# A planned kernel for four graph layers: a new VectorE-GpSimd lock and a new transfer queue in the planner, with new stage times

## The chip, the cores and the metric

The kernel runs on one NeuronCore of a Trainium2 chip. Its engines run side by side, each with its own queue of instructions served in order: TensorE (PE in the profile, its weight loads PEld), VectorE (DVE), ScalarE (ACT), GpSimd (POOL), and SyncE (SP), which here issues nearly all transfers. The metric is the device time of one execution in microseconds (us), as a median of runs. The kernel before took 2754.69 us (median of 3, from 2750.09 to 2756.34).

## The reference

There are 128 graphs of 128 nodes with 256 features (`x`, float32) and an integer adjacency matrix each (`adj`). Four layers follow, each inside `x = layernorm(x + layer(x, adj))`:

```
layer 0   e_k = leaky_relu((x * a_k) @ x.T), k = 0..3; alpha = softmax(e_k where adj == k+1, else -9e15); alpha @ x
layer 1   relu(x @ W_upd + mean over incoming edges of (x @ W_msg) + bias)
layer 2   three times: m = h @ weight[i]; agg = (adj != 0).T @ m; h = GRU(agg, h)
layer 3   Wh = x @ W; e = leaky_relu(f_i + f_j); softmax over edges; elu(alpha @ Wh)
```

The GRU's gates are `r = sigmoid(i_r + h_r)`, `z = sigmoid(i_z + h_z)`, `n = tanh(i_n + r * h_n)` and `h = (1 - z) * n + z * h`. All is float32.

## The kernel before

Graphs are taken in 32 groups of four, so that most tiles are 128 partitions by 512 columns. A group passes the stages `loading`, `layer0`, `layer1`, `step0`, `step1`, `step2` (the three GRU steps) and `layer3`. The gate products of the GRU use a seven-product scheme on two-by-two blocks (`gate`, line 753), the sums for it being made by `sums` (line 731): on GpSimd for the hidden state (`t_h`) and on VectorE for the aggregate (`t_m`). ScalarE and VectorE take the partial results out of PSUM (`q`, `t_r`, `t_i`, `t_z`). Transposes go mostly through VectorE's blockwise transpose into `z`, one transfer to DRAM (`turn`, line 487) and four transfers back (`back`, line 492): this is how `probT`, `x1T`, `hT`, `hn`, `rT` and `xc` come about. Layer norms use `statistics` (line 519): VectorE makes mean and variance, adds epsilon (`rstd`, four columns), GpSimd raises it to the power -0.5 (`rstd` again), and VectorE makes `shift`, also four columns. `normalise` then runs mostly on ScalarE.

No operation is issued as it is written. Every call is recorded as an `Op` (`Engine.__getattr__`, line 186) with its buffers, its dependences, a duration from a cost function for its engine (`pe_cost` to `sp_cost`, lines 244 to 280), and `lasts`, after which its result can be read. A planner, at the end of the function, then imitates the machine: it keeps a time at which each engine is free, asks `start_of` (line 1005) when each ready operation could start, takes the engine that can start first, and among its operations that could start by then issues the one with the earliest due time. All instructions of the main part are therefore issued from line 228, which is the line that the profile names for nearly everything.

The due times (`nominal`) come from `paced` (line 330): group g's stage lies at g times `PERIOD` plus a pair in `TIMES`, moved by a table `HEAD` for the first six groups and `TAIL` for the last six. A stage's due times are spread evenly over its operations. `EAGER` and `RUSH` move urgent operations ahead. Due times only rank operations: the planner never waits for one. About six groups are in flight at a time, since a group's stages reach from about 250 us before to 240 us after its own multiple of `PERIOD`.

Two rules of the planner stand at the centre of the change. The first is a lock between VectorE and GpSimd. An operation with `holds` set keeps the other engine's `holds` operations from starting until shortly before its end (`held`, lines 1008 and 1052). Before, VectorE's operations hold if neither output nor a wide input is in PSUM and they have two inputs of more than four columns, or are of the `FAST` forms (tensor_scalar and kin) with an output of more than four columns; `rstd`, `shift` and `ninv`, with four columns, do not. GpSimd's hold if they are a memset or have two inputs of more than four columns. The second is the landing of a transfer: a constant by tile from `LANDING` (2.4 us if not listed), plus `DMA_SLACK`, counted from its issue, whatever else is in the queue.

Of the kernel before, what the change touches and what calls it, by code (L numbers as in the profile page):

```python
# [18 lines left out]
def kernel(  # L19
# [54 lines left out]
    psum = ctx.enter_context(tc.tile_pool(name="psum", bufs=4, space=bass.MemoryType.PSUM))  # L74
# [68 lines left out]
    def m_of(view):  # L143

        m = 1
        for d in view.shape[1:]:
            m *= d
        return m
# [3 lines left out]

    class Op:
        def __init__(self, engine):
            self.engine, self.calls, self.took, self.lasts, self.dma = engine, [], 0.0, 0.0, False
            self.after, self.bufs, self.waiting = {}, [], 0
            self.ready, self.nominal, self.urgent = 0.0, 0.0, False
            self.holds = False
            self.rush = 0.0

    class Engine:
# [24 lines left out]
        def __getattr__(self, name):  # L186
            def call(*args, **kw):
                op = self.group or self.record()
                named = dict(kw)
                out = [named.pop("out")] if "out" in named else [args[0]]  # L190
                rest = args if "out" in kw else args[1:]
                if "accum_out" in named:
                    out.append(named.pop("accum_out"))
                out = [v for v in out if isinstance(v, View)]
                ins = [v for v in (*rest, *named.values()) if isinstance(v, View)]
                n = max([m_of(v) for v in out + ins])
                tensors = [v for v in ins if m_of(v) > 4]
                took, lasts = self.cost(name, n, out, ins, len(ins) - len(tensors), "accum_out" in kw)
                op.lasts = op.took + lasts
                op.took += took  # L200
                op.dma = name == "dma_start"
                if self is POOL:
                    op.holds = name == "memset" or len(tensors) > 1
                elif self is DVE and name not in ("transpose", "bn_stats"):
                    op.holds = not any(v.buf.pool is psum for v in out + tensors) and (
                        len(tensors) > 1 or (name in FAST and m_of(out[0]) > 4)
                    )
                for views, writes in ((ins, False), (out, True)):
                    for v in views:
                        whole = v.buf.pool is psum  # L210
                        for other, box, wrote in v.buf.accesses:
                            if other is not op and (writes or wrote) and (
                                whole or all(a < d and c < b for (a, b), (c, d) in zip(box, v.box))
                            ):
                                other.after[id(op)] = op
                for views, writes in ((ins, False), (out, True)):
                    for v in views:
                        v.buf.accesses.append((op, v.box, writes))
                        if v.buf not in op.bufs:
                            op.bufs.append(v.buf)  # L220
                            v.buf.left += 1
                op.calls.append((name, args, kw))

            return call
# [8 lines left out]


    FAST = ("tensor_scalar", "tensor_scalar_add", "tensor_scalar_mul")
    LANDING = {"e": 5.66, "adj_in": 4.0, "x_in": 3.85, "x1T": 3.53, "way_1": 3.2, "way_2": 3.0, "xc": 3.6, "way_f": 2.0}

    def tag_of(v):
        return v.buf.tag

    def in_psum(views):
        return any(v.buf.pool is psum for v in views)
# [16 lines left out]

    def act_cost(op, n, out, ins, pointers, sums):  # L260
        if op == "dma_start":
            return 0.6, 5.0
        lasts = 0.162 + n * 0.00083 + 0.1 * pointers
        return lasts - 0.104 + (0.12 if sums else 0.0), lasts + (0.11 if sums else 0.0)

# [11 lines left out]
        return (1.2, 1.2) if n <= 256 else (2.2, 2.2)  # L277

    def sp_cost(op, n, out, ins, pointers, sums):
        return 0.55, LANDING.get(tag_of(out[0]) if out else "out", 2.4)  # L280

    PE = Engine("PE", nc.tensor, pe_cost)
    DVE = Engine("DVE", nc.vector, dve_cost)
# [3 lines left out]
    engines = (PE, DVE, ACT, POOL, SP)  # L287


    PERIOD = 81.83483  # L290
    EAGER, RUSH = 5.2365, 0.7497
    HOP, PE_HOP, SLACK, DMA_SLACK = 0.0946, 0.0838, 0.2615, 1.3152
    STAGES = ("loading", "layer0", "layer1", "step0", "step1", "step2", "layer3")
    TIMES = {
        "loading": ((-253.2780, -231.9501), (-180.9657, -182.6682),),
        "layer0": ((-168.5025, -107.0697),),
        "layer1": ((-62.6359, -4.7662),),
        "step0": ((-4.4948, 10.3141), (7.8309, 27.7350), (15.3585, 41.6638),),
        "step1": ((53.6280, 63.7962), (55.4424, 67.5800), (69.3938, 96.3237),),
        "step2": ((107.5318, 125.3405), (123.0192, 128.3402), (118.3669, 151.8864),),  # L300
        "layer3": ((179.8537, 241.5793),),
    }
    HEAD = (
        (-47.114, 18.617, -36.138, -28.741, -1.314, -6.344, -10.582),
        (24.334, 50.812, 17.569, -15.154, 21.237, -1.480, -6.111),
        (8.991, 0.482, 19.681, -1.325, -6.604, -1.406, -2.988),
        (-25.999, 20.490, 6.185, 5.893, -23.153, 10.547, -15.132),
        (-68.952, -1.643, -3.814, -2.005, -11.556, 1.656, 4.907),
        (153.035, -10.082, -1.797, 2.074, -6.131, -2.621, -1.970),
    )  # L310
    TAIL = (
        (-25.939, 2.926, -0.338, -2.915, -0.707, 12.085, 19.318),
        (-15.615, 8.572, 14.121, 0.973, -4.836, -7.460, 3.775),
        (16.695, 22.604, 4.276, 8.937, -5.182, 2.007, 1.764),
        (-11.456, -21.112, 0.381, -6.411, -11.631, 3.563, -8.765),
        (-90.353, -2.307, -9.971, -4.006, 15.211, 6.428, 6.000),
        (82.599, 6.878, -1.456, 4.198, -5.620, 19.044, 23.289),
    )

    def spread(start, end, pe_only=False):  # L320
# [684 lines left out]
    def start_of(op):  # L1005

        at = op.ready
        if op.holds:
            at = max(at, (POOL if op.engine is DVE else DVE).held)
        for buf in op.bufs:  # L1010
            if buf.tile is None:
                slot = slot_at(buf)
                if slot is None:
                    return None
                at = max(at, slot + HOP)
                if buf.pool is psum:

                    for other, _, _ in buf.accesses:
                        for b in other.bufs:
                            if other is not op and b.tile is None and b is not buf and slot_at(b, True) is None:  # L1020
                                return None
        return at
# [5 lines left out]
    while left:  # L1028
        best = None
        for e in engines:  # L1030
            starts = [(start_of(op), op) for op in e.ready]
            starts = [(at, op) for at, op in starts if at is not None]
            if not starts:
                continue
            at = max(e.free, min(at for at, op in starts))
            if best is None or at < best[0]:
                op = min(
                    (op for t, op in starts if t <= at),
                    key=lambda op: op.nominal - (EAGER if op.urgent and e is not PE else 0.0) - op.rush * RUSH,
                )  # L1040
                best = (at, op)
        at, op = best
        e = op.engine
        for buf in op.bufs:
            if buf.tile is None:
                take_slot(buf)
        e.issue(op)
        e.ready.remove(op)
        e.free = at + op.took
        end = at + op.lasts + (DMA_SLACK if op.dma else 0.0)  # L1050
        if op.holds:
            e.held = at + op.lasts - 0.12
        for buf in op.bufs:
            buf.left -= 1
            buf.free_at = max(buf.free_at, end)
        for other in op.after.values():
            other.waiting -= 1
            to_pe = other.engine is PE
            if e is PE and to_pe:
                ready = e.free  # L1060
            elif e is other.engine and not op.dma:
                ready = end
            else:
                ready = end + (SLACK if not other.urgent else PE_HOP if to_pe else HOP)
            other.ready = max(other.ready, ready)
            if other.waiting == 0:
                other.engine.ready.append(other)
        left -= 1
# [28 lines left out]
```

## Time and profile before

| | |
|---|---|
| median of three runs | 2754.69 us (2750.09 to 2756.34) |
| profiled execution | 2750.87 us |
| its span, first to last instruction | 2749.0 us |
| mean granted TensorE clock | 0.994 |
| TensorE busy | 2678.5 us (97%), 14,332 matmul records |
| VectorE busy | 2183.6 us (79%) |
| ScalarE busy | 1807.6 us (66%) |
| GpSimd busy | 1570.5 us (57%) |
| transfers | 288.37 MB, queue q1 busy for 50.4% of 16 engines' span |

A float32 matmul is two records, a bfloat16 one is one. Matmuls are pipelined and their ends are modelled, so that TensorE's busy share is an upper figure. In groups such as `shift<-mv,rstd`, names are tiles without their numbers, left of the arrow what is written; after the count come busy time and mean duration, then the idle time of the engine before them. In the list of waits, the columns are total time, number and longest. A wait for several semaphores is put down to the last.

### The profile page before, as it was taken

The numbers are of one execution on the slowest core, as the hardware profiler recorded it, in microseconds if no ns is written. First come the engines' busy times: TensorE is split into PE (matmuls) and PEld (weight loads), VectorE is DVE, ScalarE is ACT, GpSimd is POOL, SyncE is SP. The second block draws the span as 40 slices with busy tenths as digits, with TensorE's granted clock in tenths as the row PEclk, the third lists the DMA queues.
The fourth block names the chain that finished last, engine by engine and source line by source line (L and its number), as shares of the span: only waits on it lengthen the run. The fifth ranks groups of instructions, "written<-read, shape, count | busy, mean of one in ns | idle before, by whom it ended". The sixth has DMA issues, their size and how long they took to land. (4 is left out here: it accounts for less than half of the span.)

```text
span 2749.0 us, 45121 instructions
## 1 busy us (share of the span) xinstructions
PE 2678.5 (97%) x14332; PEld 2232.4 (81%) x14332; DVE 2183.6 (79%) x5044; ACT 1807.6 (66%) x4336; POOL 1570.5 (57%) x1546
## 2 busy tenths in 40 slices
PE   8999999999999999999999999999999999999995
PEld 5788888888888888888888888888887888887784
DVE  5777878778788877788878788878778888778875
ACT  3556666666666666766666676666766666666665
POOL 4555656555656555666555657555566555566542
PEclk9999999999999999999999999999999999999997
DMA  5545555545545555555555545555545546354432
GB/s 114 112 88 108 104 102 116 110 98 105 110 105 116 109 108 101 110 112 116 115 109 104 110 106 119 117 106 110 103 105 112 113 96 132 79 105 89 99 71 51
DMA packets 1385661, 288.37 MB, mean 105 GB/s; under 512 B 1139408, under 2 KB 1385296, under 8 KB 1385424
## 3 DMA queue, kind: packets, MB, share of 16 engines
q1 hardware_dynamic: 1382976, 283.13, 50.4%
q10 hardware_dynamic: 2448, 2.36, 0.3%
q8 instruction: 115, 1.88, 0.3%
q14 instruction: 122, 1.00, 0.1%
HBM read 168.96 MB, written 116.38 MB: 104 GB/s over the span
## 5 line engine op out<-in xcount | busy, mean ns | idle before, releaser
L228 POOL TENSOR_TENSOR t_r<-t_r,t_i 128x512 f32<-128x512 f32 x186 | 244.4, 1324 | 280.8 <-ACT t_i L228 207.5
L228 PE MATMUL gate<-t_h,w_hhT 128*128 128x256 f32 x1152 | 348.1, 386 | 5.9 <-ACT t_z L228 3.8
L228 PE MATMUL gate<-t_h,w_sh 128*128 128x256 f32 x1152 | 342.0, 383 | 4.1 <-ACT q L228 1.7
L228 PE MATMUL gate<-t_m,w_sm 128*128 128x256 f32 x1152 | 341.5, 380 | 1.0 <-DVE t_m L228 0.5
L228 PE MATMUL gate<-agT,c_gi 128*128 128x256 f32 x1152 | 340.3, 380 | 1.6 <-ACT t_z L228 0.6
L228 PE MATMUL gate<-t_m,c_gi 128*128 128x256 f32 x1152 | 340.4, 379 | 0.0
L228 PE MATMUL gate<-hT,w_hhT 128*128 128x256 f32 x1152 | 331.1, 382 | 3.9 <-ACT t_z L228 2.0
L228 POOL TENSOR_TENSOR t_d<-hT,t_n 128x512 f32<-128x512 f32 x192 | 250.8, 1319 | 45.1 <-ACT t_n L228 44.5
L228 PEld LDWEIGHTS gate<-t_h,w_hhT 128*128 128x128 f32 x1152 | 207.8, 190 | 63.8 <-issue 19.8
L228 PEld LDWEIGHTS ps<-xs,xT 128*128 128x128 f32 x2048 | 248.0, 192 | 13.4 <-ACT xs L228 3.7
L228 PE MATMUL ps<-xs,xT 128*128 128x128 f32 x2048 | 251.4, 275 | 2.6 <-ACT xs L228 1.2
L228 PEld LDWEIGHTS gate<-t_m,c_gi 128*128 128x128 f32 x1152 | 218.3, 190 | 39.3 <-issue 10.0
L228 PEld LDWEIGHTS gate<-t_h,w_sh 128*128 128x128 f32 x1152 | 208.4, 190 | 49.9 <-issue 13.8
L228 PEld LDWEIGHTS gate<-hT,w_hhT 128*128 128x128 f32 x1152 | 215.4, 190 | 39.1 <-ACT t_z L228 3.6
L228 PEld LDWEIGHTS gate<-agT,c_gi 128*128 128x128 f32 x1152 | 217.4, 190 | 34.4 <-ACT t_z L228 1.8
L228 PEld LDWEIGHTS gate<-t_m,w_sm 128*128 128x128 f32 x1152 | 217.7, 190 | 33.1 <-ACT t_i L228 1.7
L228 PE MATMUL ps<-w_um,x1T 128*128 128x512 f32 x512 | 239.7, 593 | 0.0
L228 ACT ACTIVATE q<-gate,bhn 128x256 f32<-128x256 f32 x384 | 183.7, 479 | 63.0 <-PE gate L228 60.1
L228 POOL TENSOR_SCALAR mk<-a_f 128x512 uint8<-128x512 f32 x128 | 201.2, 1579 | 38.3 <-DVE alpha L228 23.1
L228 ACT COPY t_r<-gate 128x256 f32<-128x256 f32 x288 | 107.5, 373 | 172.0 <-PE gate L228 171.1
L228 POOL MEMSET alpha<- 128x512 f32 x64 | 33.3, 520 | 324.9 <-ACT wh L228 196.4
L228 ACT COPY t_i<-gate 128x256 f32<-128x256 f32 x384 | 142.3, 371 | 110.1 <-PE gate L228 105.1
(185 smaller groups left out, 6715.1 us busy)
## 6 DMA issues: line engine op xcount, KB each, us to landing
way<-z SPq DMA_DIRECT2D x188, 256.0 KB, 2.4
way_h<-z SPq DMA_DIRECT2D x128, 256.0 KB, 2.4
hn<-way_h SPq DMA_DIRECT2D x512, 64.0 KB, 2.4
x_blocks<-in_x_dram SPq DMA_DIRECT2D x256, 64.0 KB, 2.5
x_in<-in_x_dram SPq DMA_DIRECT2D x32, 512.0 KB, 4.2
rT<-way SPq DMA_DIRECT2D x256, 64.0 KB, 2.4
way_p<-z SPq DMA_DIRECT2D x62, 256.0 KB, 2.5
probT<-way_p SPq DMA_DIRECT2D x248, 64.0 KB, 2.8
```

What stands on the lines that cost most here:

```text
L228: getattr(self.engine, name)(*[a.real() if isinstance(a, View) else a for a in args], **{k: a.real() if isinstance(a, View) else a for k, ...
```

## The change

It touches only the planner: its rules and its numbers. No operation, tile or buffer count changes. `waits` is now apart from `holds`: every GpSimd operation waits for VectorE's lock, and it holds one itself if it is a memset or has one of the two-input forms in `PAIRS`, of any width (the power in `statistics` is one). VectorE's operations wait and hold if nothing they touch is in PSUM and their form is in `PAIRS` or `FAST`, again of any width. A transfer is given a service time (`SERVED`, by tile, 0.95 us for those issued by ScalarE); the queue serves one after the other, none before 0.75 us after its issue, and the end is 1.0 us after its service plus `DMA_SLACK`. SyncE's time for an issue goes from 0.55 to 0.5 us, and `sp_cost` no longer reads `LANDING`. `PERIOD`, `EAGER`, `RUSH`, the hops, `TIMES`, `HEAD` and `TAIL` have new values.

```diff
-            self.holds = False
+            self.waits = self.holds = False
...
+                if op.dma:
+                    op.queued = 0.95 if self is ACT else service(out, ins)
+                two = name in PAIRS
                 if self is POOL:
-                    op.holds = name == "memset" or len(tensors) > 1
+                    op.waits, op.holds = True, name == "memset" or two
                 elif self is DVE and name not in ("transpose", "bn_stats"):
-                    op.holds = not any(v.buf.pool is psum for v in out + tensors) and (
-                        len(tensors) > 1 or (name in FAST and m_of(out[0]) > 4)
-                    )
+                    op.waits = op.holds = not in_psum(out + ins) and (two or name in FAST)
...
-    LANDING = {"e": 5.66, "adj_in": 4.0, "x_in": 3.85, "x1T": 3.53, "way_1": 3.2, "way_2": 3.0, "xc": 3.6, "way_f": 2.0}
-
-    def tag_of(v):
-        return v.buf.tag
+    PAIRS = ("tensor_tensor", "tensor_add", "tensor_sub", "tensor_mul", "scalar_tensor_tensor", "copy_predicated")
+    SERVED = {"e": 3.5, "x1T": 0.9, "adj_in": 1.6, "x_in": 1.6, "xc": 1.5, "way_x2": 1.5, "way_f": 0.2}
+
+    def service(out, ins):
+
+        tag = out[0].buf.tag if out else "out"
+        return 1.5 if tag == "out" else SERVED.get(tag, 0.82 if tag[:3] == "way" else 0.5)
...
         if op == "dma_start":
-            return 0.6, 5.0
+            return 0.6, 2.7
...
-        return 0.55, LANDING.get(tag_of(out[0]) if out else "out", 2.4)
+        return 0.5, 1.75 + service(out, ins)
...
-    PERIOD = 81.83483
-    EAGER, RUSH = 5.2365, 0.7497
-    HOP, PE_HOP, SLACK, DMA_SLACK = 0.0946, 0.0838, 0.2615, 1.3152
+    PERIOD = 82.02493
+    EAGER, RUSH = 5.3026, 1.3855
+    HOP, PE_HOP, SLACK, DMA_SLACK = 0.0942, 0.0830, 0.2614, 0.8331
...
-        "loading": ((-253.2780, -231.9501), (-180.9657, -182.6682),),
-        "layer0": ((-168.5025, -107.0697),),
-        "layer1": ((-62.6359, -4.7662),),
-        "step0": ((-4.4948, 10.3141), (7.8309, 27.7350), (15.3585, 41.6638),),
-        "step1": ((53.6280, 63.7962), (55.4424, 67.5800), (69.3938, 96.3237),),
-        "step2": ((107.5318, 125.3405), (123.0192, 128.3402), (118.3669, 151.8864),),
-        "layer3": ((179.8537, 241.5793),),
+        "loading": ((-247.5491, -194.0561), (-143.2722, -216.6135),),
+        "layer0": ((-168.5251, -107.0951),),
+        "layer1": ((-55.2002, 2.6695),),
+        "step0": ((-4.9084, 19.3012), (-1.4435, 21.3222), (15.5190, 41.5941),),
+        "step1": ((50.8640, 70.9820), (56.8513, 77.3906), (67.7313, 96.3666),),
+        "step2": ((107.7073, 126.4989), (122.9713, 129.9877), (118.3791, 151.2368),),
+        "layer3": ((179.8434, 241.7064),),
...
-        (-47.114, 18.617, -36.138, -28.741, -1.314, -6.344, -10.582),
+        (-126.155, 5.128, -69.803, -21.348, -13.669, -8.174, -16.851),
...
-        (82.599, 6.878, -1.456, 4.198, -5.620, 19.044, 23.289),
+        (97.074, 26.443, 18.854, 20.435, 13.060, 47.535, 73.872),
...
-        if op.holds:
+        if op.waits:
             at = max(at, (POOL if op.engine is DVE else DVE).held)
...
-        end = at + op.lasts + (DMA_SLACK if op.dma else 0.0)
+        end = at + op.lasts
+        if op.queued:
+            SP.held = max(at + 0.75, SP.held) + op.queued
+            end = SP.held + 1.0
+        if op.dma:
+            end += DMA_SLACK
```

The first row of `HEAD` and the last of `TAIL` are shown; the other ten rows change in the same way.

More of the change, by code (lines that the diff above doesn't have):

```diff
@@ L154, in __init__ @@
         def __init__(self, engine):
-            self.engine, self.calls, self.took, self.lasts, self.dma = engine, [], 0.0, 0.0, False
+            self.engine, self.calls, self.took, self.lasts, self.queued, self.dma = engine, [], 0.0, 0.0, 0.0, False
             self.after, self.bufs, self.waiting = {}, [], 0
             self.ready, self.nominal, self.urgent = 0.0, 0.0, False
-            self.holds = False
+            self.waits = self.holds = False
             self.rush = 0.0
@@ L302 @@
     }
     HEAD = (
-        (-47.114, 18.617, -36.138, -28.741, -1.314, -6.344, -10.582),
[L305 to L309, printed above, removed]
+        (-126.155, 5.128, -69.803, -21.348, -13.669, -8.174, -16.851),
@@ L310 @@
+        (80.207, 34.377, 38.524, -17.547, 20.300, -9.109, -5.064),
+        (7.408, -12.202, 25.610, 5.632, -5.558, 8.108, 7.059),
+        (-65.918, 41.138, 4.487, 5.072, -12.230, 11.065, -14.228),
+        (-137.367, -1.144, -2.252, -1.129, -3.189, 2.308, 8.092),
+        (153.242, -9.402, 11.531, 0.561, -10.941, 4.205, 0.017),
     )
     TAIL = (
-        (-25.939, 2.926, -0.338, -2.915, -0.707, 12.085, 19.318),
-        (-15.615, 8.572, 14.121, 0.973, -4.836, -7.460, 3.775),
-        (16.695, 22.604, 4.276, 8.937, -5.182, 2.007, 1.764),
@@ L315 @@
-        (-11.456, -21.112, 0.381, -6.411, -11.631, 3.563, -8.765),
-        (-90.353, -2.307, -9.971, -4.006, 15.211, 6.428, 6.000),
-        (82.599, 6.878, -1.456, 4.198, -5.620, 19.044, 23.289),
+        (27.368, -6.179, -9.810, -20.906, -9.678, 2.832, 10.136),
+        (-37.995, 0.038, 5.644, -1.049, -11.456, -16.322, -4.360),
+        (57.786, 10.690, 2.358, -3.167, -6.918, -6.271, -6.896),
+        (-15.895, -28.941, -7.001, -17.741, -17.830, -3.775, -5.809),
+        (-97.576, -12.624, -18.430, -10.462, 23.529, 14.526, 53.629),
```

## The prediction

> **What bounds the kernel now.** I read the page first: engine shares and slices.
>
> ```profile
> span 2749.0 us, 45121 instructions
> PE 2678.5 (97%) x14332; PEld 2232.4 (81%) x14332; DVE 2183.6 (79%) x5044; ACT 1807.6 (66%) x4336; POOL 1570.5 (57%) x1546
> PE   8999999999999999999999999999999999999995
> PEclk9999999999999999999999999999999999999997
> ```
>
> TensorE is the bound; only the first and last slices have visible holes. But the busy figure flatters: a matmul that starts late after a switch still counts. So I cut the span into five stages and read matmul records per microsecond.
>
> ```profile
> 0.00:137.00 137.00, 120.37 (x629) 92.38 (x630) 89.67 (x223) 65.50 (x146) 68.78 (x80) 1.00 0.53 113
> 137.00:960.00 823.00, 811.03 (x4359) 675.61 (x4358) 658.46 (x1515) 543.69 (x1302) 480.23 (x469) 1.00 0.52 106
> 960.00:2052.00 1092.00, 1091.07 (x5929) 923.92 (x5928) 887.04 (x2076) 748.93 (x1795) 645.62 (x638) 1.00 0.54 110
> 2052.00:2680.00 628.00, 614.86 (x3256) 511.27 (x3255) 508.44 (x1135) 413.43 (x1001) 358.77 (x344) 1.00 0.48 99
> 2680.00:2749.00 69.00, 41.20 (x166) 29.24 (x165) 39.97 (x98) 36.00 (x93) 17.09 (x17) 0.78 0.23 50
> ```
>
> Columns: stretch, length, busy time and count of PE, PEld, DVE, ACT, POOL, then clock, DMA share, GB/s. The middle needs 1092/5929 = 0.1842 us per record. At that rate the second stage would take 4359 x 0.1842 = 802.9 us and the fourth 599.7 us: they lose 20.1 and 28.3 us, 48.4 in all. The first and last lose some 21 and 38 by the same sum (629 x 0.1842 = 116; 166 x 0.1842 = 31), mostly start and end, where there is no other work. The middle is where the planned order has settled into one rhythm for every group; losses are where head and tail tables bend it.
>
> What TensorE waits for (stages two and four, then the last):
>
> ```profile
> PE gate L228 <- ACT t_z L228: 3.1, 7, 1.0
> PE ps L228 <- DVE rest L228: 2.0, 1, 2.0
> ...
> PE gate L228 <- ACT t_z L228: 4.1, 5, 1.5
> PE ps L228 <- DVE rT L228: 2.2, 1, 2.2
> ...
> PE ps L228 <- DVE rT L228: 3.7, 1, 3.7
> PE ps L228 <- ACT wh L228: 2.7, 1, 2.7
> ```
>
> Many short waits on VectorE or ScalarE, none large on a DMA: 4.9 us for weights at the start and 1.2 for one probT are all that counts. The 2.0 us at 530-532 has this before it on VectorE and GpSimd:
>
> ```profile
> 523.23 1.23 DVE L228 TENSOR_SCALAR rstd<-mv 128x4 f32<-128x4 f32 x1
> 526.49 1.81 DVE L228 TENSOR_TENSOR rest<-rest 128x512 bf16<-128x512 f32 x1
> 528.18 1.23 DVE L228 SCALAR_TENSOR_TENSOR shift<-mv,rstd 128x4 f32<-128x4 f32 x1
> 522.78 1.65 POOL L228 TENSOR_TENSOR t_r<-t_r,t_i 128x512 f32<-128x512 f32 x1 [1.01 <-DVE mv L228]
> ...
> 527.65 1.74 POOL L228 TENSOR_TENSOR t_d<-hT,t_n 128x512 f32<-128x512 f32 x1
> ```
>
> Two four-column operations take 1.23 us each, and lie inside GpSimd's. Their fastest take 0.13 and 0.11 us. The old planner gave them no lock (four columns fall below its limits); the new one does.
>
> ```profile
> L228 DVE SCALAR_TENSOR_TENSOR shift<-mv,rstd 128x4 f32<-128x4 f32 x126 | 59.5, 472 | 14.8 <-POOL rstd L228 14.7
> L228 DVE TENSOR_SCALAR rstd<-mv 128x4 f32<-128x4 f32 x126 | 46.8, 371 | 1.9
> L228 DVE TENSOR_SCALAR ninv<-rinv 128x4 f32<-128x4 f32 x31 | 8.8, 284 | 0.0
> ```
>
> **What the Trainium skill says.** "SBUF — State Buffer", section "Who interferes with whom": a VectorE instruction with two SBUF inputs, or a two-port tensor_scalar, shares a port with a GpSimd instruction that reads SBUF, and the later one blocks fully. The trace agrees: paired with what GpSimd ran at their start, rstd, shift and ninv lose 0.81 us on average beside GpSimd's rT, 0.77 beside t_d, 0.69 beside t_r, and 0.01 when it is idle. It disagrees for GpSimd's small power: of 62 two-input VectorE operations that began during one, none lost over 0.1 us. "DMA: Bandwidth & Descriptors", section "Two DMAs through the same engine are not ordered": descriptors of one queue start in order but overlap. The trace fits a queue served in turn only loosely: 64 KB of hn lands in a median 2.4 us, 256 KB of e in 5.7. "Perfetto Trace Analysis", section "Tensor Engine Instruction (MATMUL, LD_WEIGHTS)": matmul ends are modelled, hence my counts.
>
> **The change, part by part.** No instruction is added or removed: 14,332 matmul records, all durations, and the transfers stay. What moves is order, on all five queues, so the price is only in which waits appear.
>
> *Lock for small operations.* What they wait today: shift 59.5 - 126 x 0.14 = 41.9, rstd 46.8 - 126 x 0.15 = 27.9, ninv 8.8 - 31 x 0.13 = 4.8: 75 us of VectorE time, which the old plan believed free. The middle stage has them too: shift there takes 540 ns, 54 times, and yet TensorE loses nothing, so the cover is TensorE work queued ahead. In stages two and four shift is 15.4 + 13.1 us for 65, less 9 = 19.4 us; scaled by 75/42, some 35 us of such waits lie where TensorE does run dry. If order absorbs a quarter, 9 us come back; nothing would be 0, and all of it 35. I choose a quarter because only part of the 2.0 us stall above is due to the two small waits, and other stalls go back to large operations (t_d, rT, rest) whose lock was planned before. Behind a waiting small operation stand VectorE's gate additions and rest, then TensorE.
>
> *Lock now also waited for by GpSimd's copies and masks, and held by the power.* The first is small: mk takes 1579 ns against about 1490 undisturbed, 128 x 0.09 = 11 us on an engine that is 57% busy; its cover is that slack. The second plans 128 x 1.0 us of lock that the trace does not show; it makes the plan put other VectorE work first. Bounds: -1 to +4 us; I take +1.
>
> *SyncE's transfers in turn.* Before, each landed a constant after its issue (2.4 + 1.3 for most, 5.66 + 1.3 for e). Now for one alone: 0.75 + service + 1.0 + 0.83, so hn 3.1, e 6.1, x_in and adj_in 4.2, and eight hn end 6.6 after the first issue. Measured: hn 2.4, e 5.7, x_in 4.2, adj_in 4.5 median. Its worth to TensorE is at most its DMA waits after the start, 1.2 us, plus what consumers are planned earlier: bounds -3 to +2, I take 0. In the new order the TensorE work between a transfer's source matmul and its consumer is still long: 20.5 us at the fifth percentile for hn, 26 for x1T, 33 for hT (18.8, 28.6, 40.4 before). Past SyncE, nothing on ACT's or GpSimd's queues issues transfers after the start.
>
> *Stage times.* I compared the written orders. Cut TensorE's operations into stretches of 110 (one group): before, 14 successive stretches repeat at least three quarters of the next (9 to 22), after, 16 (7 to 22). Two more stretches in rhythm, at the loss of the unsettled ones (48.4 us over 1451/81.6 = 17.8 stretches = 2.7 us each), give 5.4 us. At the start, weight products are put before the third hn and the rest transposes, which wait for loads and banks in the trace; I take 2 us (0 to 5), as the chain behind them is no shorter. The last 29 us of TensorE work stand in nearly the same order: 0. Against it: in the middle the new order has 129 TensorE operations with 0.87 us or less of TensorE work since the matmul that their input comes from, the old 87. Those of before lose about nothing (0.00 us for most), so I take 42 x 0.05 = 2 us.
>
> Sum: -9 + 1 + 0 - 5.4 - 2 + 2 = -13.4 us. The profiled execution took 2750.87 us (1.9 around the span): 2737.5. The median of the runs shown is 3.8 higher: 2754.7 - 13.4 = 2741.3, said as **2741**.
>
> **Rivals.** *The larger gain* (chance 0.10): the order absorbs most of the 48 us, 30 or more; about 2722. For it: the middle shows that no loss is possible. *No difference* (0.20): the waits are now planned but not avoidable; VectorE is 79% busy and its 75 us of waiting stay where they were, the unsettled groups just lose elsewhere. About 2754. For it: the shift waits are as frequent in the lossless middle. *A tighter rhythm, slower* (0.15): the 42 extra tight places (matmuls right after ScalarE's copies of q, t_z and t_r, in each group) miss their input. At 13.4+2 = 15.4 us over 42, 0.37 us each cancels the gain; at 0.65 us they cost 27 and the time is 2754.7 - 15.4 + 27 = 2766. Against it: like places show no loss now. *The queue model puts transfers wrong* (within the last two): adj_in is planned at 4.2 but lands in 4.5; its consumer is over 87 us of TensorE work away, so it is hidden.
>
> **How the numbers follow.** The likeliest, the 13 us gain in a spread of 6 to 25 (2730 to 2749), has 0.55. A measurement tells about 0.2%, 5.5 us. Faster: 0.10 + 0.55 less a little of its edge, plus a little of the no-difference case, 0.65. Same: 0.19. Slower: 0.16. The range runs from the larger gain, 2722, to the tight rhythm at a little under its 0.65 us, 2764.
>
> **What would show it.** Right: the mean of rstd and shift stays over 300 ns or falls, but the stages 137-960 and 2052-2680 need fewer microseconds per record (0.186 instead of 0.189 and 0.193), and the middle stays at 0.184. The queue part right: TensorE's waits for DMAs stay under 3 us after the start. Wrong: the middle above 0.186 us per record, with PE waits on ACT q, t_z or t_r in each group; or unsettled stages that lose 48 us as before.

## The result and the profile after

The kernel after takes 2738.99 us (median of 4 runs, 2736.85 to 2739.76) where the kernel before took 2755.52 us beside it (4 runs, 2750.09 to 2757.04). The ratio is 0.9942, with a 95% interval of 0.9925 to 0.996: some 16 us faster, 11 to 21 by the interval. The profiled execution took 2739.76 us, 11.1 less than the profiled one of before. Most of the 5.4 us between 11.1 and 16.5 may be the clock of these two executions: TensorE's stood at half for 36.4 us of the one of before and for 44.6 us of the one of after, which is at most half of 8.2, or 4.1 us, of time.

The head of the profile's page of the kernel after, engine by engine:

```profile
span 2737.9 us, 45131 instructions
PE 2675.7 (98%) x14332; PEld 2232.2 (82%) x14332; DVE 2207.6 (81%) x5044; ACT 1798.1 (66%) x4336; POOL 1619.3 (59%) x1546
```

The instructions are the same in kind and number, but VectorE is busy 24 us longer than before and GpSimd 49 us; a wait for the lock lies inside an operation's busy time. So these engines seem to wait more for each other, not less, and yet the kernel is faster. The same five stages (columns as in the prediction):

```profile
0.00:137.00 137.00, 119.19 (x625) 92.00 (x626) 87.59 (x223) 65.11 (x144) 68.95 (x78) 0.96 0.52 112
137.00:960.00 823.00, 814.46 (x4386) 680.44 (x4386) 668.88 (x1530) 546.31 (x1310) 499.74 (x470) 1.00 0.54 107
960.00:2052.00 1092.00, 1089.14 (x5924) 919.48 (x5923) 915.11 (x2068) 740.99 (x1803) 673.55 (x639) 1.00 0.55 110
2052.00:2669.00 617.00, 610.14 (x3239) 509.94 (x3238) 498.19 (x1129) 409.63 (x988) 361.28 (x344) 1.00 0.51 100
2669.00:2738.00 69.00, 42.74 (x164) 30.39 (x162) 37.84 (x99) 36.09 (x93) 15.78 (x17) 0.77 0.23 51
```

Divide each length by its matmul records. The second stage went from 823/4359 = 0.1888 to 823/4386 = 0.1876 us per record, and the fourth from 0.1929 to 617/3239 = 0.1905. The middle stayed at 0.1843. The head got through 625 records instead of 629 in its 137 us, at a granted clock of 0.96 instead of 1.00.

These stretches are fixed in time, so work slides across their borders. For the sums below I therefore went over the matmul records instead: from each start to the next, less a short interval that is usual for the shape, is time that TensorE lost. How short that interval is taken shifts every row by some microseconds; the differences between rows, on which the argument rests, hardly move. Time at half clock counts as lost too. Stages are borders in TensorE's own work (110, 900, 1950 and 2560 of its 2610.5 us), near those above. Two runs of the experiments stand beside, named below:

| us that TensorE lost | head | second | middle | fourth | end | sum |
|---|---|---|---|---|---|---|
| before | 28.8 | 29.2 | 9.6 | 26.4 | 27.8 | 121.8 |
| before, small operations without a lock | 26.9 | 21.6 | 8.2 | 22.4 | 27.1 | 106.2 |
| after | 31.1 | 21.6 | 13.2 | 16.7 | 28.7 | 111.3 |
| after, small operations without a lock | 30.7 | 18.2 | 12.8 | 15.0 | 27.2 | 103.9 |

After against before: 7.6 and 9.7 us gained in the second and fourth stage, 2.3, 3.6 and 0.9 lost in the others; in sum 10.5 of the 11.1 us between the two profiled executions.

What TensorE waits for, in the second stage (first line), the fourth (second line), the middle (third), and for DMAs from 110 us up to the last stage (fourth; columns are total, number, longest):

```profile
PE gate L229 <- ACT t_z L229: 3.4, 5, 1.2
...
PE gate L229 <- ACT t_z L229: 3.9, 6, 1.1
...
PE gate L229 <- ACT q L229: 2.6, 12, 0.2
...
PE ps L229 <- DMA probT<-way_p: 0.4, 1, 0.4
```

The third is new: about one short wait for ScalarE's copy of `q` in each group of the settled middle. The waits for `rest` and `rT`, which stood second in these lists before (2.0 and 2.2 us), are gone from them.

The four-column operations, from the groups by shape:

```profile
L229 DVE TENSOR_SCALAR rstd<-mv 128x4 f32<-128x4 f32 x126 | 41.7, 331 | 2.2
...
L229 DVE SCALAR_TENSOR_TENSOR shift<-mv,rstd 128x4 f32<-128x4 f32 x126 | 26.1, 207 | 5.7 <-POOL rstd L229 5.4
...
L229 DVE TENSOR_SCALAR ninv<-rinv 128x4 f32<-128x4 f32 x31 | 6.8, 220 | 0.0
```

By the prediction's sum (busy time less 0.15, 0.14 and 0.13 us each) they wait 22.8 + 8.5 + 2.8 = 34 us instead of 75. `shift` lost most of its wait: 207 ns instead of 472. But larger operations took their places in the lock. The same view for one of them, after and then before:

```profile
L229 DVE SCALAR_TENSOR_TENSOR t_r<-t_r,q 128x512 f32<-128x512 f32 x192 | 169.9, 900 | 21.0 <-ACT t_r L229 20.9
```

```profile
L228 DVE SCALAR_TENSOR_TENSOR t_r<-t_r,q 128x512 f32<-128x512 f32 x192 | 141.5, 740 | 33.2 <-ACT t_r L228 32.7
```

That is 28 us more for this group alone. So the new order did not remove waiting; it moved it from operations that the old plan had thought free to other ones. Whether the new plan meant those waits is not shown.

### The profile page after: what moved, and what is told of

Same layout as the page of the kernel before. It is cut to its first block, busy times and chain, and to the rows that moved or that the text cites. A ratio compares the mean times of both kernels' runs of the same rounds, so it can differ in the third digit from the quotient of the medians.

```text
span 2737.9 us, 45131 instructions
## 1 busy us (share of the span) xinstructions
PE 2675.7 (98%) x14332; PEld 2232.2 (82%) x14332; DVE 2207.6 (81%) x5044; ACT 1798.1 (66%) x4336; POOL 1619.3 (59%) x1546
## 4 chain that ended last, share of the span: by engine, by line
PE 84%; DVE 8%; ACT 4%; DMA 1%; issue 1%; SPq 1%; POOL 1%; DVEq 0%; POOLq 0%; ACTq 0%
PE gate L229 57%; PE ps L229 27%; DVE t_d L229 1%; DVE hT L229 1%; DVE z L229 1%; DVE t_m L229 1%; SPq L229 1%; DVE rest L229 1%; ACT xc L229 1%; ACT t_z L229 0%; ACT xs L229 0%; DVE t_z L229 0%; DVE xb L229 0%; DMA hn<-way_h 0%; ACT alpha L229 0%
## 5 line engine op out<-in xcount | busy, mean ns | idle before, releaser
L229 POOL TENSOR_TENSOR t_d<-hT,t_n 128x512 f32<-128x512 f32 x192 | 257.4, 1349 | 43.3 <-ACT t_n L229 43.0
L229 POOL TENSOR_TENSOR rstd<-rstd,neg_half 128x4 f32<-128x4 f32 (+1 forms) x128 | 157.0, 1227 | 147.9 <-DVE rstd L229 147.0
L229 PEld LDWEIGHTS gate<-t_m,c_gi 128*128 128x128 f32 x1152 | 217.3, 190 | 30.6 <-issue 0.7
L229 POOL TENSOR_SCALAR mk<-a_f 128x512 uint8<-128x512 f32 x128 | 200.9, 1576 | 27.8 <-DVE alpha L229 18.5
```

Of the source, the lines that this page charges most:

```text
L229: getattr(self.engine, name)(*[a.real() if isinstance(a, View) else a for a in args], **{k: a.real() if isinstance(a, View) else a for k, ...
```

## The experiments

The theory from the prediction: part of the gain is lock waits of four-column operations that no longer reach TensorE, part is an order with more groups in rhythm. The rivals: the new rules are worth nothing and only the times were set better; or the rules carry all of it.

**The small waits alone.** In the kernel before, with the order of every queue unchanged, the three small operations are written as reductions of one input. They leave out the epsilon and the product with the mean, so the layer norms' values are not the reference's; the negation stays.

```diff
-        DVE.tensor_scalar_add(rstd, mv[:, :, 1], EPS)
+        DVE.tensor_reduce(rstd, mv[:, :, 1:2], AX.X, OP.max)
...
-        DVE.scalar_tensor_tensor(shift, mv[:, :, 0], -1.0, rstd, op0=OP.mult, op1=OP.mult)
+        DVE.tensor_reduce(shift, rstd.rearrange("p (n o) -> p n o", [P, n, 1], o=1), AX.X, OP.max)
...
-        DVE.tensor_scalar_mul(ninv, rinv, -1.0)
+        DVE.tensor_reduce(ninv, rinv.rearrange("p (n o) -> p n o", [P, n, 1], o=1), AX.X, OP.max, negate=True)
```

> The kernel before with its order unchanged on all five queues, but rstd, shift and ninv of the statistics written as one-input reductions, which should need no lock (rstd leaves out epsilon, shift leaves out the product with the mean: values differ, durations alone matter). Lock theory (waits of these small operations that the old plan believed free reach TensorE): rstd and shift fall below 0.2 us each, some 70 us of VectorE waiting go, and the time falls by 6 to 15 us against before, most of it in 137-960 and 2052-2680. Rival (these waits are covered, the gain of the change came from elsewhere): the waits go all the same, but the time is within 3 us of before.

Measured: 2737.07 us (2734.21 to 2739.02) against 2754.04 for before, ratio 0.994 (0.9927 to 0.9952): 17 us less, a little over the 6 to 15 expected, and far from the rival's 3. The traces have the instructions of every engine in the same sequence as before. The groups of this kernel show that the waits are gone:

```profile
L228 DVE TENSOR_REDUCE rstd<-mv 128x4 f32<-128x4 f32 x126 | 19.0, 151 | 1.9
...
L228 DVE TENSOR_REDUCE shift<-rstd 128x4 f32<-128x4 f32 x126 | 18.4, 146 | 14.7 <-POOL rstd L228 14.6
```

And its second and fourth stages:

```profile
137.00:960.00 823.00, 815.27 (x4388) 681.73 (x4388) 650.41 (x1530) 546.47 (x1312) 486.25 (x474) 1.00 0.53 107
...
2052.00:2669.00 617.00, 605.48 (x3216) 504.87 (x3215) 491.80 (x1128) 408.35 (x984) 355.51 (x344) 1.00 0.49 100
```

The second runs at 823/4388 = 0.1876 us per record, the very figure of the kernel after; the fourth at 0.1919, between before (0.1929) and after (0.1905). The table of lost time above shows where the waits had counted. In the middle 37.5 us of small waits disappeared and TensorE got 1.4 us of it; in the second and fourth stages 34.7 us disappeared and TensorE got 7.6 + 4.0. It follows that these waits cost the kernel before about 17 us, as much as the whole change brought, and that the cover in the settled middle is real.

**The same in the kernel after**, whose order is likewise kept (the planner is told that the new form is like the old one), with the same parts of the computation left out.

> The changed kernel with its order unchanged, and the same three operations as one-input reductions (same parts left out). Lock theory: the changed plan has already provided for what is left of these waits, so at most 3 us come back: 2736 to 2739. Rival (the changed plan merely has other waits, not fewer surprises): 5 us or more come back, as in the kernel before.

Measured: 2732.55 us (2732.35 to 2734.88), ratio to before 0.9928 (0.9914 to 0.9941). That is 6.4 us under the kernel after, where at most 3 had been expected: the rival was nearer. The two kernels were not timed in one session, and before was 1.5 us faster in this one (2754.04 against 2755.52); less that, 4.9 us. The two intervals against before overlap, the runs themselves do not (the lowest of after is 2736.85). Its second and fourth stages:

```profile
137.00:960.00 823.00, 816.39 (x4403) 683.63 (x4402) 665.27 (x1539) 547.82 (x1315) 501.06 (x472) 1.00 0.54 107
...
2052.00:2669.00 617.00, 608.66 (x3235) 509.12 (x3233) 491.28 (x1136) 408.35 (x986) 361.38 (x345) 1.00 0.50 100
```

So the small waits still cost some 5 to 7 us after, and the change saved 17.0 - 6.4 = 10.6 us of them by the medians, 17.0 - 4.9 = 12.1 with the sessions' difference taken off, and 15.6 - 7.4 = 8.2 by the traces. Of those 7.4, 5.1 lie in the second and fourth stages, where both traces have full clock; in the rest, half-clock stretches (44.6 us in the trace of after, 35.5 in this one) may have a part. What the order gives apart from them is the distance between the two kernels without small waits: 2737.07 - 2732.55 = 4.5 us by the medians, 2.3 by the traces, with overlapping intervals against before. By stage it is larger, and of both signs: 3.4 and 7.4 us gained in the second and fourth, 3.8 and 4.6 lost in head and middle.

**Rules and times apart.** First the new rules with all the old numbers (only `DMA_SLACK` stays new, since it belongs to the queue's formula), then the old rules with all the new numbers (`DMA_SLACK` stays old).

```diff
-    PERIOD = 82.02493
-    EAGER, RUSH = 5.3026, 1.3855
-    HOP, PE_HOP, SLACK, DMA_SLACK = 0.0942, 0.0830, 0.2614, 0.8331
+    PERIOD = 81.83483
+    EAGER, RUSH = 5.2365, 0.7497
+    HOP, PE_HOP, SLACK, DMA_SLACK = 0.0946, 0.0838, 0.2615, 0.8331
...
-        (97.074, 26.443, 18.854, 20.435, 13.060, 47.535, 73.872),
+        (82.599, 6.878, -1.456, 4.198, -5.620, 19.044, 23.289),
```

(`TIMES` and the other rows of `HEAD` and `TAIL` go back in the same way.)

> The change's rules alone: new lock, new queue with its slack of 0.8331, but PERIOD, EAGER, RUSH, hops, stage times and both tables of before. Theory that the truer rules carry the gain: 2735 to 2748. Rival, that the new stage times carry it, which were found together with the rules: 2752 or more, since the old times were set for the old rules; it may be slower than before.

Measured: 2774.52 us (2772.8 to 2775.65), ratio 1.0077 (1.0065 to 1.009). The new rules alone make the kernel some 20 us slower than before.

The other half, from the kernel before:

```diff
-    PERIOD = 81.83483
-    EAGER, RUSH = 5.2365, 0.7497
-    HOP, PE_HOP, SLACK, DMA_SLACK = 0.0946, 0.0838, 0.2615, 1.3152
+    PERIOD = 82.02493
+    EAGER, RUSH = 5.3026, 1.3855
+    HOP, PE_HOP, SLACK, DMA_SLACK = 0.0942, 0.0830, 0.2614, 1.3152
...
```

(`TIMES`, `HEAD` and `TAIL` likewise.)

> The change's stage times and tables alone, with the rules of before (old lock, old landing constants with their slack of 1.3152). Theory that the rules carry the gain: no faster than before, 2752 or more. Rival, that the times carry it: within 5 us of the changed kernel's 2739.

Measured: 2750.12 us (2746.64 to 2754.97), ratio 0.9987 (0.9981 to 0.9994): 4 us faster. Neither half alone brings more than these 4 us, and one nudge of a single number under the old rules will be seen to bring as much; the rest exists only in the two together.

**One rule taken back from the kernel after.** The lock as it was:

```diff
-                    op.waits, op.holds = True, name == "memset" or two
+                    op.waits = op.holds = name == "memset" or len(tensors) > 1
...
-                    op.waits = op.holds = not in_psum(out + ins) and (two or name in FAST)
+                    op.waits = op.holds = not in_psum(out + tensors) and (
+                        len(tensors) > 1 or (name in FAST and m_of(out[0]) > 4)
+                    )
```

> The changed kernel with the lock rule of before (four-column operations and GpSimd's single-input operations outside it), the new queue and the new stage times kept. Lock theory (the lock rule is the half that counts, since small operations made lock-free took 17 us off the kernel before): 2750 or more, with rstd and shift waiting over 0.3 us each again. Rival (the queue model is what the new stage times need): within 5 us of the changed kernel's 2739.

Measured: 2770.5 us (2767.71 to 2771.91), ratio 1.0065 (1.0053 to 1.0078). The time is as the lock theory expected, but its sign is missing. The two operations were to wait over 0.3 us each again; they wait 0.18 and 0.13:

```profile
L231 DVE TENSOR_SCALAR rstd<-mv 128x4 f32<-128x4 f32 x126 | 41.7, 331 | 1.3
...
L231 DVE SCALAR_TENSOR_TENSOR shift<-mv,rstd 128x4 f32<-128x4 f32 x126 | 34.5, 274 | 6.4 <-POOL rstd L231 6.3
```

`rstd` is where it was in the kernel after, and `shift` went from 207 to 274 ns, not back to 472. So the 31 us are not the small waits come back. Then the landings as they were:

```diff
+    LANDING = {"e": 5.66, "adj_in": 4.0, "x_in": 3.85, "x1T": 3.53, "way_1": 3.2, "way_2": 3.0, "xc": 3.6, "way_f": 2.0}
...
-            return 0.6, 2.7
+            return 0.6, 5.0
...
-        return 0.5, 1.75 + service(out, ins)
+        return 0.55, LANDING.get(out[0].buf.tag if out else "out", 2.4)
...
-        if op.queued:
-            SP.held = max(at + 0.75, SP.held) + op.queued
-            end = SP.held + 1.0
```

(with `DMA_SLACK` back at 1.3152)

> The changed kernel with the transfers of before (landing constants, issue 0.55, slack 1.3152), the new lock and the new stage times kept. Lock theory: the transfers alone are worth little, 2736 to 2746. Rival (stage times fit one set of rules alone, any rule undone breaks the fit): 2750 or more, as with the lock undone. The queue as the half that counts: 2750 or more, and the run with the lock undone stays near 2739.

Measured: 2768.08 us (2766.54 to 2769.1), ratio 1.0056 (1.0044 to 1.0069), against the lock theory's 2736 to 2746 and as the rival of the fit expected. Taken alone, each of these looks like a rule worth 30 us, twice what the change as a whole brought. The next one forbids that reading. The new lock lets GpSimd's power hold VectorE off, which the trace of before contradicted. Here the planner is told the truer thing:

```diff
-                    op.waits, op.holds = True, name == "memset" or two
+                    op.waits, op.holds = True, name == "memset" or (two and m_of(out[0]) > 4)
```

> The changed kernel, but GpSimd's four-column power no longer holds the lock in the plan (the traces show no VectorE operation that waits for it), stage times kept. A truer rule alone: 2733 to 2739. Rival (the fit of stage times to rules counts for more than the truth of one rule): 2745 or more.

Measured: 2775.03 us (2773.18 to 2775.47), ratio 1.0081 (1.0067 to 1.0094), with the new rules on old times the slowest of all, where 2733 to 2739 had been expected of a truer rule. A rule nearer to the trace costs 36 us when the times stay as they were.

**How much an order off its fit costs.** Four kernels touch no rule. Three change one number, `EAGER`: in the kernel after to 5.2365 and to 5.3226, in the kernel before to 5.3026. The fourth puts the tables `HEAD` and `TAIL` of before into the kernel after.

```diff
-    EAGER, RUSH = 5.3026, 1.3855
+    EAGER, RUSH = 5.2365, 1.3855
```

> The kernel after, with all its rules and all its times but one: the allowance EAGER goes from 5.3026 back to 5.2365, so nothing that the planner knows of the lock or of SyncE is touched, and the order of the instructions changes all the same. Theory that the times are fitted to one set of rules, and that any nudge takes the order off its fit: 2760 to 2775 us, as dear as taking back the lock rule (2770.5) or the landings (2768.1), and then those two losses say nothing on the rules themselves. Rival, that the rules themselves carry those losses: this kernel stays near the kernel after, 2737 to 2745 us.

Measured: 2750.9 us (2748.56 to 2753.67), ratio 0.9988 (0.9981 to 0.9994): 12 us slower than the kernel after, between the two expectations. The loss has one place, the fourth stage, where TensorE loses 30.6 us instead of 16.7. The row of that stage, of this kernel:

```profile
2052.00:2669.00 617.00, 601.65 (x3176) 500.64 (x3176) 484.14 (x1113) 402.53 (x972) 355.72 (x341) 0.99 0.49 97
```

That is 617/3176 = 0.1943 us per record; a stretch of 6.8 us at half clock in it is at most 3.4 us of the loss.

```diff
-    EAGER, RUSH = 5.3026, 1.3855
+    EAGER, RUSH = 5.3226, 1.3855
```

> The kernel after with one number changed: EAGER from 5.3026 to 5.3226; all rules and all other times stay. A second draw of what an order costs that no search has chosen under the new rules, the first (EAGER 5.2365) having given 2750.9 us. If such draws lie near the first, 2742 to 2758 us, then the kernels with one rule taken back (2768.1 to 2775.0 us) stand out by 10 us or more, and the rules themselves carry part of their losses. If the draws scatter widely, 2760 to 2775 us, those losses cannot be told from the loss of the fit.

Measured: 2741.88 us (2740.67 to 2744.19), ratio 0.9958 (0.9944 to 0.9971), 3 us over the kernel after.

```diff
-    EAGER, RUSH = 5.2365, 0.7497
+    EAGER, RUSH = 5.3026, 0.7497
```

> The kernel before, with all its rules and times but one: EAGER goes from 5.2365 to 5.3026. Theory of the fit: slower than before by 5 to 20 us (2760 to 2775 us), which is then what an order of the old rules costs that no search has chosen. Rival: within 5 us of before (2750 to 2759 us).

Measured: 2750.24 us (2745.61 to 2753.67), ratio 0.9986 (0.9979 to 0.9993): 4 us faster than before. The theory of the fit fails on this one nudge of the old rules; the kernel before sat on no sharp best in this number.

```diff
-        (-126.155, 5.128, -69.803, -21.348, -13.669, -8.174, -16.851),
+        (-47.114, 18.617, -36.138, -28.741, -1.314, -6.344, -10.582),
...
-        (97.074, 26.443, 18.854, 20.435, 13.060, 47.535, 73.872),
+        (82.599, 6.878, -1.456, 4.198, -5.620, 19.044, 23.289),
```

> The kernel after, with the tables HEAD and TAIL of the kernel before; PERIOD, the steady TIMES, EAGER and all rules stay new. Theory that the gain sits in the groups outside the repeating middle: TensorE loses time in the stages 137 to 960 us and 2052 to 2680 us, whose groups these tables time (0.1876 and 0.1905 us per record in the kernel after, back to 0.189 and 0.193 or more), the middle stays at 0.184 us per record, and the time goes to 2755 to 2772 us. Rival, that the steady times carry the gain: 2737 to 2745 us.

Measured: 2769.04 us (2768.04 to 2769.47), ratio 1.0056 (1.0043 to 1.0069). Its second and fourth stages:

```profile
137.00:960.00 823.00, 811.16 (x4356) 677.74 (x4355) 665.21 (x1516) 545.70 (x1299) 491.09 (x467) 1.00 0.53 106
...
2052.00:2669.00 617.00, 597.50 (x3137) 494.86 (x3137) 484.69 (x1102) 400.37 (x970) 342.26 (x331) 0.99 0.50 98
```

TensorE loses 5.3 us more in the second stage and 22.0 more in the fourth, while the middle stays at 12.2 (after: 13.2), as the theory of the tables expected. They carry as much as either rule seemed to.

All orders together, with the waits of small operations in the second and fourth stages, where they can count:

| kernel | us | small waits there | TensorE lost, second + fourth |
|---|---|---|---|
| before | 2755.5 | 34.7 | 55.6 |
| old rules, new times | 2750.1 | 30.0 | 47.7 |
| before, other `EAGER` | 2750.2 | 36.3 | 55.2 |
| after | 2739.0 | 21.1 | 38.3 |
| after, `EAGER` 5.3226 | 2741.9 | 21.3 | 42.2 |
| after, `EAGER` 5.2365 | 2750.9 | 13.1 | 49.9 |
| after, old landings | 2768.1 | 19.4 | 55.6 |
| after, old tables | 2769.0 | 27.1 | 65.6 |
| after, old lock | 2770.5 | 28.0 | 69.1 |
| new rules, old times | 2774.5 | 22.2 | 54.1 |
| after, power without lock | 2775.0 | 19.5 | 70.8 |

The third column does not follow the second: the order with the fewest small waits takes 2750.9 us, and one with 19.5 us of them takes 2775.0. The fourth column follows the time in the main, and where it doesn't (new rules with old times, old landings), the middle pays: TensorE loses 24.8 and 20.6 us there instead of 13.2. Part of the fourth column may be clock: the trace of the kernel with the power without lock has 20.4 us at half clock in its fourth stage, at most 10.2 us of its 70.8. How many such waits there are says little; what they cost depends on whether TensorE runs dry behind them, and here only taking them away inside one order showed that.

What stays open: the worth of each rule by itself. The kernel after and its two nudges of `EAGER` took 2739 to 2751 us, and taking back a rule 2768 to 2775, so these stand out; but swapping tables, with every rule in place, costs as much. Only new times set for each set of rules could tell, and that was not tried.

**A version without the small waits that leaves nothing out.** From the kernel after, its order kept: `mv` has four columns per graph, (power, mean, variance, epsilon), so that `rstd` is the sum of a pair, `shift` the negated product of a pair, and `ninv` a negated maximum of one. Each is a reduction of one input.

```diff
-            DVE.bn_aggr(mv[:, b, :], st)
-        DVE.tensor_scalar_add(rstd, mv[:, :, 1], EPS)
+            DVE.bn_aggr(mv[:, b, 1:3], st)
+            if b == 0:
+                ops[-1].calls.append(("memset", (mv[:, :, 3], EPS), {}))
+        DVE.tensor_scalar_add(rstd, mv[:, :, 2], EPS)
+        ops[-1].calls[:] = [("tensor_reduce", (rstd, mv[:, :, 2:], AX.X, OP.add), {})]
...
+        ops[-1].calls[:] = [("tensor_reduce", (shift, mv[:, :, :2], AX.X, OP.mult), dict(negate=True))]
...
```

(Left out are the wider `mv`, the place of `rstd` in its first column, and `ninv`.)

> The changed kernel in its own order on every queue, with rstd, shift and ninv as one-input reductions that compute the right values: rstd as the sum of the pair (variance, epsilon), shift as the negated product of the pair (power, mean), ninv as a negated maximum; the epsilon is set by a four-column memset on VectorE after the first aggregate of each layer norm, 128 more small VectorE instructions. Lock theory: like the version that left parts out, 2732 to 2736, faster than both kernels. Rival: the memset takes the lock or its time (0.06 us or more each) gives the gain back: 2738 or more.

Measured: 2734.86 us (2734.01 to 2735.62), ratio to before 0.9937 (0.9925 to 0.9949). That is 4.1 us under the kernel after, 2.0 when the difference of before in the two sessions (2753.46 against 2755.52) is taken off; the intervals against before overlap. The traces bear the gain out where both have full clock: TensorE loses some 3.7 us less in the second and fourth stages together. The groups of this kernel show the price of the form:

```profile
L232 DVE TENSOR_REDUCE mv<-mv 128x4 f32<-128x8 f32 x126 | 19.9, 158 | 2.2
...
L232 DVE TENSOR_REDUCE shift<-mv 128x4 f32<-128x8 f32 x126 | 18.1, 144 | 5.8 <-POOL mv L232 4.8 <-POOL hu L232 0.8
...
L232 DVE MEMSET mv<- 128x4 f32 x126 | 7.8, 62 | 0.0
```

The first line is `rstd`, which now lies in `mv`; it takes 158 ns and `shift` 144. The added memsets take 7.8 us of VectorE. Whether they are what keeps this kernel 2 us behind the one that leaves parts out (2732.55) is not shown; the runs of the two overlap. It has the lowest median of the kernels that leave nothing out.

## Why the prediction was right, point by point

The time, 2741 us, is 2 us from the measured 2739.0, and the 13.4 us of the sum stand between the 11.1 us of the profiled executions and the 16.5 of the medians. The terms fared differently.

*Lock for small operations, -9.* Right in place and nearly in size: 8.2 us by the traces, 10.6 to 12.1 by the medians. The factor of a quarter behind it was wrong in its parts, and the errors cancelled, which was luck. By the traces the waits cost 15.6 us in all: 11.6 us, a third of the 34.7, in the two unsettled stages, and 4.0 in the others, which the sum had left out. Of that cost the new order took back about half by the traces (three fifths or more by the medians), not all: 6.5 us in the two stages, a fifth of the 34.7, and 1.7 in the others. The reading that the settled middle hides its waits held: 37.5 us taken away there gave 1.4.

*Power held, masks waiting, +1.* Not settled. The power without its lock cost 36 us rather than bringing one, which says that the times suit the rule, not that the rule is good. The waits of GpSimd's copies and masks were not tried apart.

*SyncE's queue, 0.* Nothing speaks against the cover named, long TensorE work between a transfer's source and its consumer: the waits for DMAs after the start fell from 1.2 to 0.4 us. What the rule does to the order could not be measured apart.

*Two more stretches in rhythm, -5.4.* The sign came out right, too small, and the reason does not hold. Without small waits the new order gains 3.4 + 7.4 = 10.8 us in the second and fourth stages over the old. But counting stretches that repeat does not tell a fast order from a slow one. Counted in the traces by stretches of 448 matmul records, one group each, the kernel before has 14 that repeat three quarters of the next and the kernel after 17 (the prediction counted 14 and 16 in the written orders), and the kernel after with the old lock has 17 as well and takes 2770.5 us; with the power without lock it has 15, more than before, and takes 2775.0. Giving each stretch 2.7 us found the sign by luck. What makes one order lose less than another in these stages stays open.

*Start, -2.* Not seen: TensorE lost 2.3 us more in the head. The clock there was 0.96 of full speed, against 1.00 before. The records show 10.2 us at half clock in the head, so up to 5 us may be the clock, and a gain of 2 us may lie beneath. The clock may in turn belong to the order: each of the ten profiled kernels with the new rules, whole or with one taken back, has such a stretch near 40 or 76 us, and none of the four with the old rules has one there (two have one at 13 us). The kernel with `EAGER` at 5.3226, which has the same tables and 3.4 us at half clock, lost 28.0, about what before did (28.8). No kernel with the new tables lost 2 us less than before in the head.

*Tight places in the middle, +2.* Right mechanism and near in size, differently composed: 3.6 us more lost in the middle, of which 2.6 are 12 waits of 0.22 us for ScalarE's `q`, about one in a group, rather than 42 of 0.05. The wait is still there without small waits (2.4 us), so it is of the order. The slower rival had this place right but needed 0.65 us for each of 42 waits.

One sign named in advance could not fail: that the mean of `rstd` and `shift` "stays over 300 ns or falls" holds whatever happens. It fell to 331 and 207 ns. The others, the records per microsecond in each stage, carried the verdict: from 0.1888 and 0.1929 they fell to 0.1876 and 0.1905, towards the expected 0.186 but short of it, and stayed at 0.184 in the middle.

The rival of no difference failed on the same two stages. Its argument, that VectorE's waiting stays, was true of VectorE as a whole (it is busy 24 us longer) and still decided nothing: in the middle, 37.5 us of waits taken away gave TensorE 1.4, in the second and fourth stages 34.7 gave 11.6.

## What to carry to other kernels

A planner's rules and its due times have to be judged together: here a rule nearer to the machine cost 36 us, and all the new rules some 20, while the times stayed as they were, and undoing one rule cost twice what the whole change had brought. To price a wait, keep the order and take the wait out of the instruction, by a form that doesn't take the lock; adding up waits across orders did not follow the time here. And before teaching a planner to avoid a lock for many small operations, see whether they can be written so that they don't take it.

## What the runs showed of the hardware

- A reduction of one input over four columns on VectorE took no lock: `rstd` and `shift` took 151 and 146 ns, where the tensor_scalar and scalar_tensor_tensor forms took 371 and 472 ns in the same order. None of them took more than 0.05 us over the shortest, whatever GpSimd ran at its start; before, the other forms had lost up to 1.1 us. A reduction over pairs (128x8 into 128x4), as a sum or a negated product, took 158 and 144 ns.
- TensorE's clock fell to half for stretches of 3.4 to 10.2 us in the head of some executions (in sum 10.2 us in the profiled one of after, none in that of before), with the same instructions on TensorE but for their order. What brings them on is not shown.
